# A hybrid scan kernel: the gate moved behind its slot's scan, the norm's variance a slot later, expert pairs packed one slot closer

## The chip, the cores and the metric

The kernel runs on one core of one Trainium2 chip, as one launch. The metric is the device time in microseconds, the median of several executions. The whole computation is in fp32.

## The reference, cut to what matters

The input is x of shape (2, 256, 64, 64): two batches, 256 channels, 4096 positions. Layer 0 adds to x a selective scan (Mamba) over the positions of the group-normed x. Layer 1 layer-norms the tokens, adds a forward and a backward Mamba with 512 inner channels each, and then adds a mixture of 8 experts: every expert is a three-layer MLP of 256 x 256 matrices with a batch norm and a ReLU behind the first two, and a softmax over the experts, computed from the mean of both batches, weighs them.

```python
# one Mamba, for inner channel d and state s
h = h * exp(dt[d] * A[d, s]) + dt[d] * x[d] * B[s]      # scan over positions
y[d] = sum_s h[d, s] * C[s] + x[d] * D[d]
out = (y * silu(z)) @ W_out
# experts
n = layernorm(t)                                        # over channels
t = t + sum_e w[f, e] * (relu(bn(relu(bn(n @ W1[e])) @ W2[e])) @ Wo[e])
```

## The kernel before, in words

Positions are cut into 8 chunks of T = 512. A job is one Mamba on one batch: layer 0 (256 inner channels, nj = 2 tiles of 128), the forward and the backward one of layer 1 (nj = 4). The six jobs follow one another, batch 0 first; 48 steps (a job and a chunk) in all. The backward job walks the chunks from 7 to 0.

The scan is done in quads. A quad g covers one tile of 128 channels and 4 of the 16 states, laid out as 128 partitions times 4 groups of 512 positions. There are 640 quads; 8 quads (n = 0 to 7, two channel tiles of 4 quads) make a group. Every quad has two halves h, and each half is one **slot**: 1280 slots in all, 16 to a step of layer 0 and 32 to a step of layer 1. In a quad POOL multiplies dt x by B (`emit_b`, L654, into a buffer bq, of which there are six); ACT computes the decay da into PSUM (L664, a slot ahead, two buffers); DVE runs the recurrence over half a quad (`emit_scan`, L690); the product with C is made by DVE (`emit_times_c`, L699) or, for the quads n = 0, 2, 5 and in every second group half of n = 4, by POOL (L714 copies the carried state, L715 multiplies); PE then sums the states into y (`emit_sum`, L723), which frees bq. y has a single PSUM buffer: it is opened by a matmul with the skip weights D (`emit_skip`, L730) and closed by the gate on DVE (`emit_gate`, L742), which writes y silu(z) into sz. `SUMS` gives the slots (n, h) in which the quads of a group are summed; -1 is the last quad of the group before.

The order on every engine is the order in which the main loop issues, slot by slot. In each slot it issues, in this order: DMAs on SP, (before the change) the gate, the skip, prepared matmuls ("pe"), the sums, expert matmuls ("pe2"), the carries and the next decay on ACT, prepared ACT work, the scan, prepared DVE work ("dve"), the C product, and POOL's work. Work around the scan is put into slots by hand: `SLOTS` says how many slots ahead of a step its input projection, convolution, x projection, softplus (dt) and z are made. `norm` and `features` spread a layer norm over slots: mean on PE, centre on DVE, squares on ACT, variance on PE (L804 in `features`), a root on ACT (L179, L180), a product on DVE (L809), a store on SP. `features` does this for the experts' norm, one chunk at a time, behind each step of a backward job, and notes in `ready` from which slot the chunk's experts may run.

An expert **pair** here is one expert on one chunk of one batch. `experts` plans as many pairs as fit into the scan stage: it walks the slots, counts the matmuls that PE and the activations that ACT have in each (`sl.count`, `sums_in`, `PE_ROOM`, `ACT_ROOM`), and places each layer's two output halves (L912 matmul, L921 or L923 eviction) where there is room. `follows` gives the earliest slot: a layer's next pair may start some slots behind the last use of the layer's weights, whose tile ew has one buffer. The load of the next weights (L932) is put on SP three slots behind that last use. Results go to DRAM as u (L942).

Behind the scan stage comes the tail. Pairs that were not done early run there on PE, chunk after chunk (L1201 for the first two layers, L1220 for the third, summed over experts in PSUM), each weighed on DVE (L1212) before its third layer. For each chunk there is side work, spread over the pairs of the chunk ahead of it: load n (L1086), add both batches (L1108), logits on PE (L1115), the softmax, the broadcast of the weights wb (L1146), the bias (L1163, L1164, L1166), and for each early pair a load of u (L1170), a product with its weight (L1171) and an addition to x (L1172) on DVE; the finished chunk is stored (L1175). The side work of the first chunk starts at its third pair.

Of the kernel before, what the change touches and what calls it, by code (L numbers as in the profile page):

```python
# [49 lines left out]
KC = C // P  # L50
# [11 lines left out]

POOL_HALF = (4, 0)

SUMS = {(0, 0): (-1,), (2, 0): (0, 1), (4, 0): (2, 3), (5, 1): (4,), (7, 0): (5, 6)}
POOL_AT = {0: "b3", 1: "c0 b4", 2: "b5", 3: "c2 b6", 4: "b7", 5: "h4 b8", 6: "c5 b9", 7: "b10"}
HUGE = 1e37

# [63 lines left out]
def hybrid_kernel(ctx: ExitStack, tc: tile.TileContext, a: dict, out: bass.AP):  # L132
    nc = tc.nc
# [11 lines left out]
    one_col, eps3, eps5, eps10, huge = (columns[:, k : k + 1] for k in range(5))  # L145
# [22 lines left out]
    nf_dram = [drp.tile([P, NCH, KC, T], F32, name=f"nf_dram{b}") for b in range(NB)]  # L168
# [9 lines left out]
    def rsqrt(dst, src, eps, scale=1.0):  # L178
        nc.scalar.activation(dst, src, AF.Ln, bias=eps, scale=scale)  # L179
        nc.scalar.activation(dst, dst, AF.Exp, scale=-0.5)  # L180
# [5 lines left out]
    with ExitStack() as st:  # L186
# [30 lines left out]
        sl = Slots()  # L217
# [467 lines left out]
        def emit_scan(g, h):  # L685
            i, j, sg = at(g)
            job, c = steps[i]
            d = da[g, h].rearrange("p q t -> p (q t)")
            b = bq[g][:, 2 * h : 2 * h + 2, :].rearrange("p q t -> p (q t)")
            nc.vector.tensor_tensor_scan(  # L690
                b if on_pool(g, h) else d, d, b,
                job.h[:, j, sg, 2 * h : 2 * h + 1] if c else 0.0, ALU.mult, ALU.add,
            )
# [46 lines left out]
        def emit_gate(i, j):  # L740
            sz = cks[i]["sz", j]
            nc.vector.scalar_tensor_tensor(sz, y.pop((i, j)), 0.5, sz, ALU.mult, ALU.mult)  # L742
# [38 lines left out]
        def features(b, c, v, s0):  # L781

            featured.add((b, c))

            def mean():
                v["ps"] = psp.tile([P, T], F32, tag="ps", name=f"fmean_{b}{c}")
                for k in range(KC):
                    nc.tensor.matmul(
                        v["ps"], mean_w, v["x"][:, k, :], start=(k == 0), stop=(k == KC - 1)
                    )  # L790

            def centre():
                v["cen"] = wk.tile([P, KC, T], F32, tag="cen", name=f"fcen_{b}{c}")
                nc.vector.tensor_tensor(v["cen"], v["x"], over_channels(v["ps"]), ALU.subtract)

            def square():
                for k in range(KC):
                    v["sq", k] = wk.tile([P, T], F32, tag="th", name=f"fsq_{b}{c}{k}", bufs=3)
                    nc.scalar.activation(v["sq", k], v["cen"][:, k, :], AF.Square)

            def variance():
                v["var"] = psp.tile([P, T], F32, tag="ps", name=f"fvar_{b}{c}")
                for k in range(KC):
                    nc.tensor.matmul(  # L804
                        v["var"], mean_w, v["sq", k], start=(k == 0), stop=(k == KC - 1)
                    )

            def divide():
                nc.vector.tensor_tensor(v["cen"], v["cen"], over_channels(v["var"]), ALU.mult)  # L809

            for d, queue, fn in (
                (0, "pe", mean), (1, "dve", centre), (2, "act", square), (3, "pe", variance),
                (4, "act", lambda: rsqrt(v["var"], v["var"], eps5)), (5, "dve", divide),
                (6, "sp", lambda: nc.sync.dma_start(nf_dram[b][:, c, :, :], v["cen"])),
            ):
                sl.put(s0 + d, queue, fn)
            sl.count(s0, 2, 0, (1,))
            sl.count(s0 + 1, 0, 2)
            sl.count(s0 + 3, 2, 2, (2,))
            ready.append((s0 + 8, b, c))  # L820

        def scales():

# [23 lines left out]
        def experts():  # L847

            last = 2 * nq - 6
            banks = sorted(sl.banks, key=lambda r: r[0])  # L850

            def fits(slot):

                at = sum(b[0] <= slot for b in banks)
                both = banks[:at] + [(slot, slot + 1, 0)] + banks[at:]
                return all(
                    both[k - 3][1] + both[k][2] <= both[k][0] for k in range(max(3, at - 2), min(len(both), at + 4))
                    if at in range(k - 3, k + 1)
                )

            def sums_in(slot):
                n, h = divmod(slot % 16, 2)
                return 1.25 * len(SUMS.get((n, h), ())) + (1 if (n, h) in ((1, 1), (5, 1)) else 0)

            todo = [(at, b, c, e) for at, b, c in sorted(ready) for e in range(E)]
            behind = act_behind = 0.0
            times = [[], [], []]

            def follows(l):

                k, m = divmod(len(times[l]), KC)
                if k == len(todo):
                    return None
                waits = [(l - 1, k * KC + 1, 2)] if l else []
                if m:
                    waits.append((l, k * KC, 0))
                elif k:

                    waits.append((l, k * KC - 1, 6 if l == 0 and todo[k][-1] == 0 else 5))
                    if l < 2:  # L880
                        waits.append((l + 1, k * KC - 1, 0))
                if any(n >= len(times[w]) for w, n, _ in waits):
                    return None
                return max([todo[k][0] + 3] + [times[w][n] + d for w, n, d in waits])

            for slot in range(last):
                behind = max(0.0, behind) + sl.products.get(slot, 0) + sums_in(slot) - PE_ROOM
                act_behind = max(0.0, act_behind) + sl.acts.get(slot + 1, 0) - ACT_ROOM
                for l in (2, 1, 1, 0, 0):
                    at = follows(l)  # L890
                    if at is None or slot < at:
                        continue
                    if behind + 2 > PE_BEHIND or act_behind + 1.3 > ACT_BEHIND or not fits(slot):
                        break
                    banks.insert(sum(b[0] <= slot for b in banks), (slot, slot + 1, 0))
                    times[l].append(slot)
                    behind += 2
                    act_behind += 1 if l == 2 else 1.3
            put = [
                (*item[1:], [times[l][k * KC + m] for l in range(3) for m in range(KC)])  # L900
                for k, item in enumerate(todo) if (k + 1) * KC <= len(times[2])
            ]
            emit_experts(put)
# [58 lines left out]
        ready = []  # L962
# [47 lines left out]
        done = []  # L1010
        for g in range(nq):
            i, jp, n = quads[g]
            for h in range(2):
                slot = 2 * g + h
                sl.run(slot, "sp")
                flush(slot)

                if (n, h) in ((1, 0), (5, 0)) and done:
                    emit_gate(*done.pop(0))

                if (n, h) in ((1, 1), (5, 1)):
                    emit_skip(i, 2 * jp + n // SG)
                sl.run(slot, "pe")
                for m in SUMS.get((n, h), ()):
                    if g - n + m >= 0:
                        emit_sum(g - n + m)
                sl.run(slot, "pe2")
                if (n, h) in ((0, 0), (4, 0)) and g:
                    done.append(at(g - 1)[:2])

                if slot:
                    emit_carry(*divmod(slot - 1, 2))
                emit_decay(*divmod(slot + 1, 2))
                if (n, h) in ((0, 0), (4, 0)):
                    emit_diagonal(i, 2 * jp + n // SG)
                sl.run(slot, "act")

                sl.run(slot, "dve0")
                emit_scan(g, h)
                sl.run(slot, "dve")  # L1040
                if not on_pool(g, h):
                    emit_times_c(g, h)

                if h == 0:
                    for what in POOL_AT.get(n, "").split():
                        m = g - n + int(what[1:])
                        if what[0] == "c":
                            emit_times_c_quad(m)
                        elif what[0] == "h":
                            if on_pool(m, 0):  # L1050
                                emit_times_c_quad(m, SG // 2)
                        else:
                            want_b(m)
                sl.run(slot, "pool")
            in_order()
# [335 lines left out]
```

## Time and profile before

| | |
|---|---|
| median of 3 runs | 5206.82 us (5206.63 to 5207.61) |
| the profiled execution | 5213.06 us |
| its span, first to last instruction | 5211.3 us |
| mean granted TensorE clock | 0.918 |
| busy: PE, DVE, ACT, POOL | 4298.0, 4584.8, 3681.8, 4410.2 us |
| scan stage | from about 44 us (first POOL product) to about 4542 us (last output projection) |
| tail | from 4545 us to the end |
| early pairs of 128 | 74 |

The durations in the profile are those of the profiled execution. Busy time is an average over stages with different limits, so a row of the windows view (one stretch of time, busy microseconds of PE, weight loads, DVE, ACT and POOL, then the clock, the DMA share and GB/s) is the view to start from. A number in square brackets in the timeline is the time for which the engine had been idle just before the instruction, and what ended that.

### The profile page before, as it was taken

The page shows a single profiled execution, that of the slowest core. Times are in us where ns is not written, and L with a number is a line of the kernel's source. Part 1 is how long each engine was busy: PE and PEld are TensorE (multiplying, and loading weights), DVE is VectorE, ACT ScalarE, POOL GpSimd, SP SyncE. Part 2 cuts the span into 40 slices and gives each one's busy share as a digit, 9 for nine tenths or more (in the row PEclk, how much of TensorE's full clock was granted, in tenths as well). Part 3 has the DMA queues.
Part 4 walks back from the last instruction along what each step waited for, and adds up shares of the span by engine and source line. Part 5 has one row for each costly group of instructions (what it writes and reads, how often), then busy time and mean ns, then how long its engine had stood idle before and what let it go on. Part 6 is the DMA issues. An engine that isn't in the chain of part 4 may idle for free. (4 is left out here: it accounts for less than half of the span.)

```text
span 5211.3 us, 47295 instructions
## 1 busy us (share of the span) xinstructions
PE 4298.0 (82%) x14920; PEld 1488.2 (29%) x14920; DVE 4584.8 (88%) x3083; ACT 3681.8 (71%) x7462; POOL 4410.2 (85%) x1438
## 2 busy tenths in 40 slices
PE   5777666766668888888888888888999989689999
PEld 1222212222222333332222332322333333234444
DVE  6998999999999999998989999999999999746333
ACT  5777777777767888887887888788788888522332
POOL 5998999999999999998989999999999999611010
PEclk8778888888889999999999999999999999899999
DMA  4444433344434554555555544445544455354322
GB/s 175 146 165 164 162 134 126 130 156 148 140 135 159 187 186 166 181 174 185 197 177 182 178 169 169 164 159 194 184 171 163 163 184 178 115 194 154 111 103 77
DMA packets 314731, 834.47 MB, mean 160 GB/s; under 512 B 35240, under 2 KB 102064, under 8 KB 272496
## 3 DMA queue, kind: packets, MB, share of 16 engines
q1 hardware_dynamic: 310768, 806.15, 44.5%
q0 software_dynamic: 3712, 25.30, 1.2%
q8 instruction: 118, 1.93, 0.1%
q14 instruction: 133, 1.09, 0.1%
HBM read 647.18 MB, written 184.16 MB: 160 GB/s over the span
## 5 line engine op out<-in xcount | busy, mean ns | idle before, releaser
L654 POOL TENSOR_TENSOR bq<-rxdt,bc 128x2048 f32<-128x2048 f32 x640 | 2892.9, 4542 | 34.8 <-issue 17.4
L664 ACT ACTIVATE da<-rdt,w_a 128x512 f32<-128x512 f32 x2560 | 1756.8, 686 | 113.6 <-DVE bq L690 67.8
L690 DVE TENSOR_TENSOR_SCAN da<-da,h_state,bq 128x1024 f32<-128x1024 f32 x664 | 1559.5, 2349 | 38.7 <-ACT da L664 27.3
L715 POOL TENSOR_TENSOR bq<-bq,bc 128x2048 f32<-128x2048 f32 (+1 forms) x280 | 1179.6, 4213 | 22.5
L723 PE MATMUL y<-bq,stack 128*32 128x512 f32 x5120 | 779.4, 687 | 362.1 <-POOL bq L715 337.2
L690 DVE TENSOR_TENSOR_SCAN bq<-da,h_state,bq 128x1024 f32<-128x1024 f32 x456 | 1052.3, 2337 | 27.9 <-ACT da L664 27.8
L699 DVE TENSOR_TENSOR bq<-da,bc 128x1024 f32<-128x1024 f32 x760 | 928.2, 1221 | 18.7
L912 PE MATMUL e<-eh,ew 128*128 128x512 f32 x1184 | 582.4, 621 | 60.5 <-DVE sp L513 20.5
L709 ACT COPY h_state<-da 128x2 f32<-128x2 f32 x759 | 119.3, 157 | 687.5 <-DVE bq L699 685.4
L675 ACT ACTIVATE bq<-h_state,bq,a 128x1 f32<-128x1 f32 x1120 | 429.9, 384 | 0.5
L723 PEld LDWEIGHTS y<-bq,stack 128*32 128x32 f32 x5120 | 144.9, 118 | 935.1 <-POOL bq L715 458.6
L1205 ACT ACTIVATE h<-hp,of,sc 128x512 f32<-128x512 f32 x216 | 167.7, 777 | 345.0 <-PE hp L1201 328.5
L414 PE MATMUL xs<-nx,w_in 128*128 128x512 f32 x640 | 320.1, 630 | 36.8 <-DVE xc L466 20.7
L414 PE MATMUL z<-nx,w_in 128*128 128x512 f32 x640 | 326.2, 638 | 23.7 <-DVE sp L513 16.9
L912 PEld LDWEIGHTS e<-eh,ew 128*128 128x128 f32 x1184 | 212.4, 193 | 422.3 <-issue 194.5
L912 PE MATMUL e<-en,ew 128*128 128x512 f32 x592 | 290.5, 622 | 47.3 <-DVE fcen L809 21.5
L452 PE MATMUL conv<-xs,w_conv 64*64 64x512 f32 x2560 | 320.5, 608 | 4.6 <-DVE sp L513 3.7
L761 PE MATMUL o<-sz,w_out 128*128 128x512 f32 x640 | 306.7, 620 | 0.0
L923 ACT ACTIVATE eh<-e,of,sc 128x512 f32<-128x512 f32 x296 | 223.7, 769 | 37.9 <-PE e L912 36.7
L517 POOL TENSOR_TENSOR xdt<-sp,xc 128x512 f32<-128x512 f32 x160 | 203.4, 1275 | 53.3 <-DVE sp L513 53.3
L501 PE MATMUL dt<-dbc,w_dt 64*128 64x512 f32 x320 | 197.2, 701 | 44.5 <-ACT dbc L488 27.7
L730 PE MATMUL y<-xc,w_d 128*128 128x512 f32 x320 | 181.0, 649 | 60.8 <-DVE sz L742 51.3
(138 smaller groups left out, 5043.0 us busy)
## 6 DMA issues: line engine op xcount, KB each, us to landing
rxdt<-xdtd SPq DMA_DIRECT2D x160, 1024.0 KB, 6.4
rdt<-dtd SPq DMA_DIRECT2D x160, 1024.0 KB, 6.3
bc<-bcd SPq DMA_DIRECT2D x384, 256.0 KB, 3.2
dtd<-sp SPq DMA_DIRECT2D x160, 256.0 KB, 3.5
xdtd<-xdt SPq DMA_DIRECT2D x160, 256.0 KB, 3.4
ew<-in_W SPq DMA_DIRECT2D x148, 256.0 KB, 4.8
u<-eu SPq DMA_DIRECT2D x74, 512.0 KB, 3.5
u<-u SPq DMA_DIRECT2D x74, 512.0 KB, 4.0
```

The source lines that it names most:

```text
L414: nc.tensor.matmul(ps, job.w["in", half][:, k, j * P : (j + 1) * P], rhs, start=(k == 0), stop=(k == KC - 1),)
L452: nc.tensor.matmul(v[r][64 * col : 64 * col + 64, :], job.w["conv"][rows, 2 * jp + j, k, :], ck["xs", jp][rows, j, k : k + T] if k < 4 els ...
L654: nc.gpsimd.tensor_tensor(bq[g], ck["rxdt", j], over_groups(ck["bc", 0, sg]), ALU.mult)
L664: nc.scalar.activation(da[g, h][:, k, :], cks[i]["rdt", j][:, q, :], AF.Exp, scale=steps[i][0].w["a"][:, j, q * SG + sg : q * SG + sg + 1],)
L675: nc.scalar.activation(bq[g][:, q, 0:1], job.h[:, j, sg, q : q + 1], AF.Identity, scale=cks[i]["a0", j][:, h, sg : sg + 1], bias=bq[g][:, ...
L690: nc.vector.tensor_tensor_scan(b if on_pool(g, h) else d, d, b, job.h[:, j, sg, 2 * h : 2 * h + 1] if c else 0.0, ALU.mult, ALU.add,)
L699: nc.vector.tensor_tensor(bq[g][:, two, :], d, cks[i]["bc", 1, sg].rearrange("p (o t) -> p o t", o=1).to_broadcast([P, 2, T]), ALU.mult,)
L715: nc.gpsimd.tensor_tensor(b, b, cks[i]["bc", 1, sg].rearrange("p (o t) -> p o t", o=1).to_broadcast([P, groups, T]), ALU.mult,)
L723: nc.tensor.matmul(y[i, j][q * CG : (q + 1) * CG, :], stack, bq[g][:, q, :], start=False, stop=(sg == SG - 1),)
L761: nc.tensor.matmul(v[m], job.w["out"][:, j, m * P : (m + 1) * P], ck["sz", j], start=False, stop=(j == job.nj - 1),)
L912: nc.tensor.matmul(ps, ew[l][:, k, m * P : (m + 1) * P], key[x][:, k, :], start=(k == 0), stop=(k == KC - 1),)
L923: nc.scalar.activation(key[dst][:, m, :], key["ps", l, m], AF.Relu, bias=of[:, l, e, m : m + 1], scale=sc[:, l, e, m : m + 1],)
```

## The change

Four edits, all of them in the order of work:

1. `emit_gate` is issued behind `emit_scan` of its slot, not at the slot's start. The skip, which opens y again, goes from slots (1, 1) and (5, 1) to (2, 0) and (6, 0), and the sum of quad 4 goes with it; `sums_in` follows.
2. In `features` the variance stands two slots behind the squares instead of one. Root, product, store and the slot from which the chunk is ready move by one.
3. In `follows` a layer's next pair may start four slots behind the last use of its weights, not five (six stays where a new chunk begins).
4. What the planner makes of it: 77 pairs are done early instead of 74. Three more pairs of chunk 6 of batch 1 (experts 2, 3 and 4) leave the tail, so that chunk has 3 pairs left there instead of 6, and 13 additions of early results instead of 10.

```diff
-SUMS = {(0, 0): (-1,), (2, 0): (0, 1), (4, 0): (2, 3), (5, 1): (4,), (7, 0): (5, 6)}
+SUMS = {(0, 0): (-1,), (2, 0): (0, 1), (4, 0): (2, 3), (6, 0): (4,), (7, 0): (5, 6)}
...
-                (0, "pe", mean), (1, "dve", centre), (2, "act", square), (3, "pe", variance),
-                (4, "act", lambda: rsqrt(v["var"], v["var"], eps5)), (5, "dve", divide),
-                (6, "sp", lambda: nc.sync.dma_start(nf_dram[b][:, c, :, :], v["cen"])),
+                (0, "pe", mean), (1, "dve", centre), (2, "act", square), (4, "pe", variance),
+                (5, "act", lambda: rsqrt(v["var"], v["var"], eps5)), (6, "dve", divide),
+                (7, "sp", lambda: nc.sync.dma_start(nf_dram[b][:, c, :, :], v["cen"])),
...
-            sl.count(s0 + 3, 2, 2, (2,))
-            ready.append((s0 + 8, b, c))
+            sl.count(s0 + 4, 2, 2, (2,))
+            ready.append((s0 + 9, b, c))
...
-                return 1.25 * len(SUMS.get((n, h), ())) + (1 if (n, h) in ((1, 1), (5, 1)) else 0)
+                return 1.25 * len(SUMS.get((n, h), ())) + (1 if (n, h) in ((2, 0), (6, 0)) else 0)
...
-                    waits.append((l, k * KC - 1, 6 if l == 0 and todo[k][-1] == 0 else 5))
+                    waits.append((l, k * KC - 1, 6 if l == 0 and todo[k][-1] == 0 else 4))
...
-                if (n, h) in ((1, 0), (5, 0)) and done:
-                    emit_gate(*done.pop(0))
-
-                if (n, h) in ((1, 1), (5, 1)):
+                if (n, h) in ((2, 0), (6, 0)):
                     emit_skip(i, 2 * jp + n // SG)
...
                 emit_scan(g, h)
+
+                if (n, h) in ((1, 0), (5, 0)) and done:
+                    emit_gate(*done.pop(0))
                 sl.run(slot, "dve")
```

## The prediction, made before the changed kernel ran

> **What bounds the kernel now.** I read the windows view first, cut by stage: the rows give length, then busy time of PE, weight loads, DVE, ACT and POOL.
>
> ```profile
> 40.00:560.00 520.00, 367.17 (x1302) 107.66 (x1302) 459.85 (x301) 376.49 (x768) 471.84 (x152) 0.80 0.48 166
> 560.00:1650.00 1090.00, 755.19 (x2893) 232.39 (x2895) 1067.34 (x700) 787.82 (x1652) 1084.25 (x345) 0.85 0.40 143
> 2230.00:2740.00 510.00, 444.89 (x1582) 147.58 (x1580) 456.95 (x295) 415.95 (x835) 456.95 (x145) 0.96 0.54 185
> 3700.00:4480.00 780.00, 703.79 (x2518) 245.20 (x2510) 759.66 (x488) 628.01 (x1298) 769.11 (x244) 0.96 0.50 173
> 4660.00:4760.00 100.00, 91.14 (x218) 38.95 (x217) 73.18 (x62) 26.62 (x36) 15.54 (x11) 0.98 0.51 176
> ```
>
> There are three regimes. In the layer-1 scans (second and fourth row) POOL is busy 99% and DVE 97 to 98%: POOL's multiplications set the pace, one step of 32 slots every 109.5 us, and a stall of PE or ACT costs nothing. In the two layer-0 scans (40:560, 2230:2740) POOL is at 90% and DVE at 88 to 90%: neither is full, so somebody waits on the path. After about 4545 PE works through the remaining expert pairs. Next, who waits in the first layer-0 scan (engine, line, releaser, us in total, times, longest), and below it the whole run:
>
> ```profile
> POOL h_state L714 <- DVE bq L690: 15.8, 11, 2.0
> DVE sz L742 <- PE y L723: 16.5, 7, 4.7
> ...
> DVE sz L742 <- PE y L723: 45.4, 37, 4.7
> PEld fvar L804 <- ACT fsq L799: 77.6, 30, 5.1
> PE fvar L804 <- ACT fsq L799: 57.8, 16, 4.3
> ```
>
> The gate (L742) holds DVE's queue until PE has summed y; the scan behind it is late, and POOL's product, which reads that scan, waits too. The timeline shows it:
>
> ```profile
> 218.25 0.69 DVE L742 SCALAR_TENSOR_TENSOR sz<-y,sz 128x512 f32<-128x512 f32 x1 [2.73 <-PE y L723]
> 218.86 4.58 DVE L690 TENSOR_TENSOR_SCAN bq<-da,h_state,bq 128x1024 f32<-128x1024 f32 x2
> 223.51 0.19 POOL L714 COPY h_state<-bq 128x4 f32<-128x4 f32 x1 [1.48 <-DVE bq L690]
> ```
>
> The reader should see that this pair is the only place where a wait that the change touches reaches the engine that sets the pace.
>
> The tail is read from its timeline:
>
> ```profile
> 4627.95 2.33 POOL L1108 TENSOR_TENSOR nm<-n,n 128x1024 f32<-128x1024 f32 x1 [12.24 <-DMA n<-nf_dram]
> 4662.14 3.36 DVE L1172 TENSOR_TENSOR x<-x,u 128x1024 f32<-128x1024 f32 x1 [8.01 <-POOL x L1166]
> 4677.93 1.23 DVE L1171 TENSOR_TENSOR u<-u,wb 128x1024 f32<-128x1024 f32 x1 [5.37 <-DMA u<-u]
> 4691.19 5.40 PE L1220 MATMUL y<-h,Wo 128*128 128x512 f32 x8 [3.64 <-DVE h L1212]
> ```
>
> Between 4590 and 4710 DVE, adding the early pairs' results (L1171 and L1172, 1.22 + 1.23 us a pair), holds PE, not the other way round.
>
> **What the Trainium skill says.** "PSUM — Partial Sum Buffer", Engine vs sequencer instructions: the queues of ScalarE, VectorE and GpSimd are strict FIFO. The trace agrees: the scan behind the gate at 218.25 starts only after it. "SBUF — State Buffer", Who interferes with whom: a DVE instruction with two SBUF inputs contends with a GpSimd one that reads SBUF. It agrees in the tail (the L1172 add takes 3.36 beside POOL, 1.23 alone); in the scan stage DVE reads one operand from PSUM, and POOL's product keeps 4.54. "DMA: Bandwidth & Descriptors", Issuing engines are not separate DMA queues: all issuers share the 16 DMA engines; that matters for the tail below. "Perfetto Trace Analysis", Optimization Strategy: the most contended engine may differ by regime; the windows say so here.
>
> **The change part by part.**
> *Gate behind its slot's scan.* No instruction is added. DVE runs scan, gate instead of gate, scan, so y gets one scan (2.35 us) more; a stall s becomes s - 2.35 or nothing. The stalls of the first layer-0 scan in the timeline are 4.73, 2.56, 2.73, 1.37, 2.13, 2.67 and 0.34: 16.5 in all, 3.3 left, 13.2 saved. In the second they are 1.00, 1.17, 4.03, 2.60 and 0.34: 9.1, 1.9 left, 7.2 saved. The other 25 (20 us) lie where POOL is full, or at the end: the last gate (2.05) is issued outside the loop and stays. POOL waits on DVE for 15.8 us in the first scan and 28.4 in the second, so there is room for the gain to arrive; ACT, the next in line (10.9 us of DVE's waits for da in the first), takes some. I count 11 and 5 (0 to 13.2, 0 to 7.2), and 1 for the rest (0 to 4). Behind the moved gate stand the slot's C product (1.22) and the next scan: they come 0.68 later than the scan, no later than before.
> *Skip (L730) one slot on, sum of quad 4 with the skip.* The skip must follow the gate, which is later by a scan; a slot is about 3.46 us, so PE's wait there (51 + 25 us for L742) does not grow. In layer 0 the sum now stands behind the convolution (40 matmuls, 4.5 us): its bq buffer comes free some 8 us later. POOL takes that buffer after a C product and a B product of another quad, 9 us; so nothing, at worst 1 us on each of 16 steps if PE is late. I take 0.5 in all.
> *Variance two slots behind its squares.* PE waited for the squares 77.6 us as the loader, of which 57.8 are matmul idle (the same stretches, not a sum). In layer-1 scans POOL covers that: 0 us, except at the very end, where the norm's last DVE step waited 1.62 on it; I count 1. The square's buffers (tag th) are held a slot longer: ACT's softplus waited 14.4 us in 9 for them and may wait as much again, covered by ACT's own waiting for DVE (685 us at L709); 0, at worst 5. The store and the read of that norm move one slot on SP; its first reader is a pair that the planner places after it.
> *Next pair four slots on instead of five: 77 pairs early, not 74.* Into the scan stage go 3 x 24 traced matmuls (0.43 us apart, 31 us of PE), 3 x 6 evictions on ACT (four of 0.77, two of 0.57: 12.7 us) and 12 DMAs on SP. PE has 76 us idle in 3700:4480, 25 of them the very wait for the squares that goes (in 3800:4400); ACT has 152. Cover: POOL. The weights' tile has one buffer: its load is issued three slots behind the last use, lands in 4.6 us (median), and the next use came two slots after the issue, now one. By the two plans 23 of 228 loads are that tight; each may hold PE 1 to 3 us, some 45 us of PE, and whatever SP queues behind the load waits for PE as it does now (231 us at L932). Hidden in layer 1; in layer 0 a handful count: 1.5 (0 to 8).
> *In the tail* three pairs go: 4.29 + 2.84 + 3.43 = 10.6 us each in the chain, 31.7 in all. I count none of it. Chunk 6 keeps 3 pairs, and all its side work (13 adds, not 10, and the routing of chunks 7 and 5) is now issued in one piece between its third pair and chunk 5. Routing of chunk 5 hangs on its n, which POOL sums at 4627.95 after the same DMAs as before; so PE can't begin chunk 5 before about 4636 (it began at 4646.4): 10 us instead of 31.7. Then DVE: three adds more (7.3) and a weighing fewer before chunk 5's first add, which until now waited 8.0 for POOL. 7.3 - 1.1 - 8.0 = -1.8, but x of chunk 5 is loaded behind the additional u and four weight loads, and the broadcast wb now meets the u loads on the shared DMA engines: +1 to +5. Net +1 (-2 to +6). From the weighing ahead of 4691.19 on, order and work are as before.
>
> Sum: -11 - 5 - 1 + 0.5 - 1 + 1.5 + 1 = **-15.0**. Against the profiled execution (span 5211.3, 5213.06 with what lies around it) 5198.1; the median shown is 6.2 below that, so **5192**, 0.29% under 5206.82.
>
> **Rivals.**
> *Tail counted in full.* If PE set the tail, 31.7 would come on top: 5160. PE is busy 91 of 100 us in 4660:4760, which speaks for it; the 3.64 ahead of 4691.19 and the missing pairs to fill 4604 to 4636 speak against. Half of it gives 5176.
> *No gain.* ACT takes the gate's place in layer 0 (it already ends 13.8 us of DVE's waits in the first): -0 to -8, 5199 to 5207. The 2.35 us of freed DVE time usually end in POOL's waits for DVE, which speaks against.
> *Slower.* PE falls behind in the last layer-1 scan: it is 90% busy there, gets 21 us more and most of the tight reloads. It decides once PE's 76 idle us are used up, so that y comes later than the gate's extra 2.35 us; then each of 16 steps loses about 1.5 us: +24, with 9 of the layer-0 gain left, is 5222. The load there, 21 us and a third of the 45, stays under half of the 76, so I give it little.
>
> **How the numbers follow.** Main case 0.62 (5184 to 5200, likeliest 5192); tail at least half 0.12; no gain 0.14; slower 0.12. The range 5174 to 5210 takes in the half tail and the no-gain case. A measurement of this kernel tells about 0.2% (10.4 us) from no change: the main case is faster by more in four fifths (0.50), with the tail 0.62, and a part of the middle 0.02: faster 0.64, same 0.25, slower 0.11.
>
> **What would show it.** L742's wait in 40:560 falls from 16.5 to about 3, in 2230:2740 from 9 to 2, POOL's wait at L714 falls with it, and the scan stage ends some 16 us earlier. The waits at L804 nearly vanish without a gain in layer 1: the step stays at 109.5 us. The time from the last scan to the end stays within a few us of now, with PE idle between 4604 and 4636 and again ahead of chunk 5's second y. It is wrong if the tail shortens by 20 us or more, if the layer-1 step changes, or if L912 waits for its weights by tens of us while POOL waits with it.

## The result, and the profile after

The changed kernel takes **5185.24 us** (median of 5 runs, 5181.76 to 5189.58) against 5206.82. The ratio is 0.9955, 95% interval 0.9943 to 0.9967, so it is 0.45% faster. The profiled execution took 5185.24 us, its span 5183.5. The forecast of 5192 (5174 to 5210) holds it. In good part that is luck: the gain of gate and variance and the cost of the packing were both put far too low, and the two errors, of opposite sign, met in the sum. The experiments separate them.

The windows view of the changed kernel, in the columns of before (length, busy time of PE, weight loads, DVE, ACT and POOL, clock, DMA share, GB/s):

```profile
40.00:560.00 520.00, 368.28 (x1338) 117.20 (x1337) 470.94 (x309) 382.27 (x783) 482.19 (x154) 0.82 0.49 167
2230.00:2740.00 510.00, 441.99 (x1582) 148.11 (x1582) 469.17 (x306) 428.87 (x857) 473.79 (x154) 0.96 0.56 191
3700.00:4480.00 780.00, 699.14 (x2496) 244.53 (x2497) 752.72 (x482) 625.42 (x1301) 763.30 (x242) 0.96 0.51 172
```

POOL is busier in both layer-0 scans (482.19 instead of 471.84 us, 473.79 instead of 456.95), which is where most of the time came from. In the last layer-1 scan it is *less* busy than before (763.30 of 780, was 769.11), which the main case of the prediction did not allow for. The granted clock there is 0.96 as before, so it is not the clock. The waits in the first layer-0 scan (waiting engine and line, releaser, us in total, times, longest):

```profile
POOL h_state L714 <- DVE bq L690: 9.7, 6, 2.1
...
DVE sz L742 <- PE y L723: 3.0, 3, 2.5
```

The gate's wait fell from 16.5 to 3.0, as worked out. POOL's wait for the scan fell by less, from 15.8 to 9.7. Of the gate's fall only what reaches POOL can be time of the kernel, as POOL sets the pace: these 6.1 us, and 10.3 if all that POOL stood idle in the stretch is counted (its busy time rose by that much). The same pair of instructions as before, in the timeline:

```profile
215.33 0.69 DVE L742 SCALAR_TENSOR_TENSOR sz<-y,sz 128x512 f32<-128x512 f32 x1
...
219.37 0.19 POOL L714 COPY h_state<-bq 128x4 f32<-128x4 f32 x1
```

The 2.73 us ahead of the gate and the 1.48 ahead of POOL's copy are gone. One wait of the whole run:

```profile
PE fvar L804 <- DVE sp L513: 55.8, 11, 5.3
```

PE's wait at the variance (L804) did not vanish. It waited 57.8 us for ACT's squares before; it now waits 55.8 us for DVE's L513.

To see where along the program time is won or lost I list the start of every 16th or so gate (L742; there are 160, the last one right behind the loop) minus the start of the same gate in the profile of before, and the time from the last gate to the end. Gates 1 to 16 are those of the first layer-0 scan, 81 to 96 those of the second, 97 to 128 those of batch 1's forward job and 129 to 160 those of its backward job, the last scan.

| kernel | gate 16 | 76 | 96 | 112 | 128 | 144 | 160 | last gate to end, us |
|---|---|---|---|---|---|---|---|---|
| before | 0 | 0 | 0 | 0 | 0 | 0 | 0 | 679.7 |
| changed | -8.6 | -13.3 | -28.7 | -31.1 | -28.6 | -24.4 | -24.3 | 676.2 |
| gate only | -11.7 | -13.7 | -25.0 | -27.2 | -25.7 | -28.6 | -29.3 | 677.9 |
| variance only | -4.6 | -3.8 | -12.6 | -13.0 | -10.0 | -12.0 | -15.7 | 682.7 |
| packing only | -3.7 | 0.0 | -0.2 | +2.5 | +5.0 | +4.2 | +4.1 | 678.1 |
| gate and variance | -9.8 | -12.8 | -26.8 | -30.4 | -30.4 | -33.0 | -37.3 | 674.0 |

The rows below the second are those of the first four experiments. The profiled execution of before was a long one (6.2 us above its median), and "variance only" and "packing only" have its program up to gate 16: some 4 us of every row there are run to run. Ten kernels of this document have the moved gate and the same program up to gate 16; there they lie on average 10.0 us ahead of before (8.5 to 11.7), the three without it 2.8 (0 to 4.6), so the move is worth about 7 us in the first scan. Later columns are best read against each other, and to some 3 us only. The changed kernel wins 15.4 us between gates 76 and 96 (a later kernel, which differs from it in the tail alone, wins 11.9) and then gives 4.3 back between 128 and 160, the last scan, where gate and variance without the packing win 6.9 more.

The tail is 3.5 us shorter, for three pairs fewer. Its timeline:

```profile
4577.35 3.58 PE L1115 MATMUL lt<-wr,nm 128*128 128x8 f32 x16 [8.67 <-POOL nm L1108]
...
4600.14 2.33 POOL L1108 TENSOR_TENSOR nm<-n,n 128x1024 f32<-128x1024 f32 x1 [11.85 <-DMA n<-nf_dram]
...
4602.53 3.58 PE L1115 MATMUL lt<-wr,nm 128*128 128x8 f32 x16 [18.85 <-POOL nm L1108]
...
4608.66 5.71 PE L1201 MATMUL hp<-n,W 128*128 128x512 f32 x8
...
4666.37 5.94 PE L1220 MATMUL y<-h,Wo 128*128 128x512 f32 x8 [7.05 <-DVE h L1212]
```

PE stands 8.67 and 18.85 us for the sum of both batches' n, begins chunk 5 at 4608.66, and then waits for DVE's weighing (4.35 us at 4646.77, 7.05 at 4666.37), which stands behind the additions.

### The profile page after: what moved, and what is told of

Read it like the earlier page. It is cut to its first block, busy times and chain, and to the rows that moved or that the text cites. A ratio compares the mean times of both kernels' runs of the same rounds, so it can differ in the third digit from the quotient of the medians.

```text
span 5183.5 us, 47326 instructions
## 1 busy us (share of the span) xinstructions
PE 4289.2 (83%) x14920; PEld 1486.0 (29%) x14920; DVE 4580.7 (88%) x3086; ACT 3678.8 (71%) x7468; POOL 4409.0 (85%) x1438
## 4 chain that ended last, share of the span: by engine, by line
DVE 20%; PE 15%; ACT 9%; issue 4%; POOL 4%; DMA 2%; SPq 0%; DVEq 0%; POOLq 0%; ACTq 0%
DVE da L690 10%; PE hp L1201 6%; DVE bq L699 5%; ACT da L664 4%; PE y L1220 3%; DVE bq L690 2%; POOL bq L654 2%; PE e L912 2%; PE conv L452 1%; POOL bq L715 1%; ACT bq L675 1%; PE y L723 1%; ACT eh L923 1%; DVE xc L466 1%; DMA u<-u 1%
## 5 line engine op out<-in xcount | busy, mean ns | idle before, releaser
L690 DVE TENSOR_TENSOR_SCAN bq<-da,h_state,bq 128x1024 f32<-128x1024 f32 x456 | 1059.3, 2338 | 28.5 <-ACT da L664 28.4
L723 PE MATMUL y<-bq,stack 128*32 128x512 f32 x5120 | 761.1, 688 | 329.3 <-POOL bq L715 304.6
L912 PE MATMUL e<-eh,ew 128*128 128x512 f32 x1232 | 604.1, 621 | 69.2 <-DVE sp L513 13.5
L414 PE MATMUL z<-nx,w_in 128*128 128x512 f32 x640 | 322.9, 637 | 19.3 <-DVE sp L513 11.9
L730 PE MATMUL y<-xc,w_d 128*128 128x512 f32 x320 | 194.8, 694 | 54.2 <-DVE sz L742 53.9
L690 DVE TENSOR_TENSOR_SCAN da<-da,bq 128x1024 f32<-128x1024 f32 x96 | 219.5, 2286 | 6.3 <-ACT da L664 3.6
```

The lines of the kernel that those rows point to most:

```text
L414: nc.tensor.matmul(ps, job.w["in", half][:, k, j * P : (j + 1) * P], rhs, start=(k == 0), stop=(k == KC - 1),)
L690: nc.vector.tensor_tensor_scan(b if on_pool(g, h) else d, d, b, job.h[:, j, sg, 2 * h : 2 * h + 1] if c else 0.0, ALU.mult, ALU.add,)
L723: nc.tensor.matmul(y[i, j][q * CG : (q + 1) * CG, :], stack, bq[g][:, q, :], start=False, stop=(sg == SG - 1),)
L912: nc.tensor.matmul(ps, ew[l][:, k, m * P : (m + 1) * P], key[x][:, k, :], start=(k == 0), stop=(k == KC - 1),)
```

## The experiments

Theory after the result: gate and variance gain in the layer-0 scans, the packing loses in the last layer-1 scan because of its evictions (the activations by which ACT takes the experts' results out of PSUM), and the tail is held by its side work. Rivals: the tight reload of weights (the load lands only just before its use), the mere amount of expert work, or PE's pairs in the tail. Ratios are to runs of the kernel before on the same chip; "gain" is what the ratio lacks to 1, times 5206.8.

**Each part alone, and two together.** The first takes edit 1 of the change, the second edit 2, the third edit 3 with the number of pairs fixed, the fourth edits 1 and 2.

```diff
 # third kernel
-                    waits.append((l, k * KC - 1, 6 if l == 0 and todo[k][-1] == 0 else 5))
+                    waits.append((l, k * KC - 1, 6 if l == 0 and todo[k][-1] == 0 else 4))
...
-            ]
+            ][:77]
```

> Only the gate, the skip and the sum of quad 4 are moved; 74 pairs as before. Theory (the gate's stall in the layer-0 scans pays): nearly the whole gain is here. The first layer-0 scan gets about 11 us shorter, the second at least 7, the layer-1 scans and the tail stay within 3 us: 5185 to 5190. Rival (the variance's wait or the packing pays in the second layer-0 scan, where the changed kernel gained 13 us): the first layer-0 scan gains 11, the second under 4: 5193 to 5197.

Measured: 5182.77 us, ratio 0.9948 (0.9931 to 0.9964), a gain of 27 us (19 to 36), more than expected. The layer-1 scans do not stay within 3 us: between gates 16 and 76, and 96 and the last, it wins 6.3.

> Only the variance of the experts' norm is two slots behind its squares; 74 pairs. Theory: PE's wait at L804 goes, POOL covers it, so 5203 to 5208; at most 2 us come from the end of the scan stage. Rival (the wait at L804 is what held PE, ACT and then the gate at the start of the second layer-0 scan): 4 to 9 us less, 5198 to 5203, all of it between 2240 and 2740 us.

Measured: 5200.3 us, ratio 0.9983 (0.9976 to 0.9990), a gain of 9 us (5 to 12). The rival of the expectation holds.

> Only the packing, four slots instead of five, cut off at 77 pairs. Theory: three pairs leave the tail, and the tail gets only 2 to 5 us shorter, because n of the next chunk and the additions on DVE hold it; in the scan stage they cost 0 to 8 us: 5202 to 5212. Rival (a pair moved is worth its 10.6 us on PE): 5175 to 5185.

Measured: 5214.67 us, ratio 1.0012 (1.0005 to 1.0018): a loss of 6 us (3 to 9), outside the 5202 to 5212 expected. None of it comes from the last scan (between gates 128 and 160 it wins 0.9): it loses 3.7 between gates 16 and 76 and 5.2 between 96 and 128. Its plan puts the pairs into other slots than that of the changed kernel.

> Gate and variance, five slots as before: the planner makes 73 pairs. Theory: like the changed kernel without its packing; the layer-0 gains are kept, the about 6 us that the changed kernel loses in the last layer-1 scans do not appear, and the tail with a pair more is 0 to 3 us longer than before: 5180 to 5187. Rival (the loss in the last layer-1 scans comes from the later variance holding the squares' buffers): that loss of about 6 us stays, 5187 to 5193.

Measured: 5169.42 us, ratio 0.9923 (0.9908 to 0.9938), a gain of 40 us, far more than expected. The loss in the last scan does not appear, though the variance is moved here too, so the squares' buffers are not its cause. The packing therefore costs the full change about 16 us (5185.24 - 5169.42), more than it costs alone; 11.2 of them lie between gates 128 and 160.

What the variance moves is two places. The first: the norm of batch 0's last chunk falls into the first slots of batch 1's layer-0 scan, where POOL isn't full. The timeline of the kernel before there:

```profile
2392.40 1.28 ACT L179 ACT_TABLE_LOAD   x1
2393.70 0.66 ACT L179 ACTIVATE fvar<-fvar,columns 128x512 f32<-128x512 f32 x1
...
2394.38 1.28 ACT L180 ACT_TABLE_LOAD   x1
...
2396.16 0.59 ACT L776 COPY xr<-o 128x512 f32<-128x512 f32 x1
...
2396.81 1.19 PE L759 MATMUL o<-xr,ident 128*128 128x512 f32 x2 [3.62 <-ACT xr L776]
...
2402.45 4.54 POOL L654 TENSOR_TENSOR bq<-rxdt,bc 128x2048 f32<-128x2048 f32 x1 [6.15 <-PE y L723]
...
2403.27 0.69 DVE L742 SCALAR_TENSOR_TENSOR sz<-y,sz 128x512 f32<-128x512 f32 x1 [4.03 <-PE y L723]
```

ACT makes the norm's root with two table loads; xr stands behind it in ACT's queue; PE waits 3.62 us for xr, and the sums behind it in PE's queue come late, so that POOL waits 6.15 for a buffer and the gate 4.03 for y. With the variance alone moved, the timeline has:

```profile
2391.65 4.54 POOL L654 TENSOR_TENSOR bq<-rxdt,bc 128x2048 f32<-128x2048 f32 x1 [0.41 <-PE y L723]
...
2392.46 0.69 DVE L742 SCALAR_TENSOR_TENSOR sz<-y,sz 128x512 f32<-128x512 f32 x1 [1.63 <-PE y L723]
```

POOL's wait fell by 5.7 us. The table agrees: variance only wins 8.8 us between gates 76 and 96. The second place is the last norm of all, at the end of the loop, which the prediction named. POOL's last wait for a scan, in the kernel before:

```profile
4515.53 0.19 POOL L714 COPY h_state<-bq 128x4 f32<-128x4 f32 x1 [3.83 <-DVE bq L690]
```

and with the variance alone moved:

```profile
4499.86 0.19 POOL L714 COPY h_state<-bq 128x4 f32<-128x4 f32 x1 [1.45 <-DVE bq L690]
```

The last eight gates take 2.5 us less with the variance alone moved, 0.2 less with the gate alone. In this kernel a tail 3 us longer takes that back.

**The last three pairs back in the tail.** The changed kernel, with

```diff
                 if (k + 1) * KC <= len(times[2])
-            ]
+            ][:74]
```

> The changed kernel with its early pairs cut at 74, so that the last three go back to the tail; the four-slot rule stays for the other 74. If the pairs hardly matter to the tail (theory, from the gate-and-variance kernel with 73 pairs, whose tail was 674.0 us against 676.2 with 77), the time stays within 4 us of the changed kernel's 5185, and the stretch from the last gate in the loop to the end within 3 us of 676. If each pair costs its 10.6 us of the chain there (rival), it is 31 us slower, about 5216. If the three pairs that were put last are what holds up the last layer-1 scan, its last gate comes some 7 us earlier and the time falls to about 5178.

Measured: 5182.14 us, ratio 0.9947 (0.9930 to 0.9963), last gate to end 679.7 us. The pairs are worth 3.5 us of tail, not 31.7. Taking them out of the scan stage gave 4.4 us at its end (last gate at 4502.89 instead of 4507.27). The changed kernel has there:

```profile
4477.27 3.75 PE L912 MATMUL e<-eh,ew 128*128 128x512 f32 x4 [6.99 <-DMA ew<-in_Wo]
...
4491.20 0.19 POOL L714 COPY h_state<-bq 128x4 f32<-128x4 f32 x1 [4.30 <-DVE bq L690]
```

PE stands 6.99 us for weights of the last pair; the variance is behind it in PE's queue, root and product come late, and POOL waits 4.30 us for the scan behind them, 1.10 in the cut. By these two traces a reload does cost at this one place, about 3 us; it was not tried apart from its pair. Up to gate 154 the cut lay within 2.2 us of the changed kernel, so the rest of the loss in the last layer-1 scan is not these pairs'.

**Evictions or reloads.** In both kernels below the planner leaves a slot after placing one half of a layer there, so that ACT never has two expert evictions in one slot. The first keeps the four slots, the second has five and so no tight reload.

```diff
                     act_behind += 1 if l == 2 else 1.3
+                    break
```

> The changed kernel with the four-slot rule kept, but the planner places at most one half of a layer in a slot, so that no slot has two or three expert evictions on ACT (68 have two and 2 have three in the changed kernel). It gets 69 pairs early, with 22 of their weights reloaded in the tight four slots (23 in the changed kernel). Read by the last gate in the loop, which lay at 4507 in the changed kernel and at 4494 with the five-slot rule. Theory (two evictions in a row on ACT make a decay late): the last gate comes at 4494 or earlier. Rival (the tight reload holds PE): it stays at 4505 to 4509. The tail has eight pairs more; up to the first four they were free, four more may cost 15 to 42 us, so the whole is expected at 5185 to 5215 whatever the verdict on the scan.

Measured: last gate at 4494.94; 5230.34 us, ratio 1.0044 (1.0029 to 1.0059).

> Gate and variance as changed, five slots between pairs, and at most one half of a layer in a slot: 66 pairs early, no tight reload and no two evictions in a slot. With the kernel before it this makes a square: evictions together or not, reload tight or not. Theory (evictions): the last gate lies with that of the one-eviction kernel with four slots, within 4 us, and before that of the gate-and-variance kernel (4494). Rival (reload): it lies with the gate-and-variance kernel, 10 us or more before the one-eviction kernel with four slots. The tail has 11 pairs more than the changed kernel's: 30 to 75 us longer, the whole 5195 to 5245.

Measured: last gate at 4491.34; 5232.96 us, ratio 1.0048 (1.0033 to 1.0063).

The scan is decided: with 22 tight reloads and no two evictions together the last gate (4494.94) lies where it lies without tight reloads (4494.33 for gate and variance, 4491.34 here). The reload is out as the cause of what every step loses. The tails are a miss on the upper side: 734.1 us for 69 pairs early, where I had expected 15 to 42 us on 676.2. With 69 pairs chunk 6 keeps all eight of its pairs, and PE is nearly full there; the window of the one-eviction kernel:

```profile
4600.00:4700.00 100.00, 96.32 (x230) 41.24 (x228) 40.18 (x37) 28.42 (x38) 10.07 (x7) 0.98 0.33 120
```

PE has 96.32 us busy of 100 in place of 81.57 in the changed kernel. The eight pairs cost about 58 us of tail (734.1 instead of 676.2), but the three more of the second kernel only another 5.7: what a pair costs there depends on what PE waits for beside it. These two kernels also have 8 and 11 pairs fewer in the scan, so the amount of work was still a rival.

**Evictions or amount of work.** As the first of them, but only from slot 1024 on, which is the last layer-1 scan:

```diff
                     act_behind += 1 if l == 2 else 1.3
+                    if slot >= 1024:
+                        break
```

> The changed kernel with the four-slot rule, at most one half of a layer in a slot from slot 1024 on (the last layer-1 scan), and free before. It has 74 pairs early and 21 tight reloads, so it stands against the cut at 74 with the same number of pairs and, but for two, of tight reloads; what differs is that one slot of the last scan has two evictions on ACT instead of 17. Theory (two evictions ahead of a decay): up to the gate at about 3630 it runs with the changed kernel, and from there to the last gate it loses nothing: last gate at 4493 to 4497, DVE's wait for da at L690 under 6 us in that scan, the whole 5171 to 5177. Rival (the amount of expert work, or the tight reload): last gate at 4502 to 4507 as in the cut at 74, the whole 5180 to 5186.

Measured: 5174.81 us, ratio 0.9933 (0.9918 to 0.9948); last gate at 4495.06, 7.8 us before that of the cut at 74 with the same number of pairs. At gate 128 it was 1.7 us ahead, so 6.1 come from the last scan. The waits of POOL and DVE from 3630 to 4400, in the cut at 74:

```profile
POOL h_state L714 <- DVE bq L690: 12.1, 10, 1.5
...
DVE bq L690 <- ACT da L664: 11.0, 7, 2.1
...
DVE da L690 <- ACT da L664: 6.5, 9, 1.8
```

and with the evictions spread:

```profile
DVE bq L690 <- ACT da L664: 8.5, 5, 2.6
...
POOL h_state L714 <- DVE bq L690: 4.7, 5, 1.5
...
DVE da L690 <- ACT da L664: 1.4, 2, 1.2
```

POOL's wait falls by 7.4 us, about those 6.1. The expectation named 6 us for DVE's first wait; it is 8.5, but three quarters of the second wait went too (17.5 to 9.9 together). Sorted by what ACT did since the decay before, 9.2 of the 17.5 us stand behind two or more expert evictions and 8.3 behind one or none; with the evictions spread it is 0 and 9.9. So the number of pairs is out: the part behind evictions that stand together went, and the rest stayed. How it looks, in the timeline of the changed kernel:

```profile
3968.93 1.41 ACT L664 ACTIVATE da<-rdt,w_a 128x512 f32<-128x512 f32 x2
3970.27 0.58 ACT L436 COPY xs<-xs 128x512 f32<-128x512 f32 x1
...
3970.98 0.58 ACT L921 COPY eu<-e 128x512 f32<-128x512 f32 x1
3971.46 0.78 ACT L923 ACTIVATE eh<-e,of,sc 128x512 f32<-128x512 f32 x1
...
3974.37 1.42 ACT L664 ACTIVATE da<-rdt,w_a 128x512 f32<-128x512 f32 x2 [1.79 <-DVE bq L690]
...
3975.82 2.35 DVE L690 TENSOR_TENSOR_SCAN bq<-da,h_state,bq 128x1024 f32<-128x1024 f32 x1 [1.48 <-ACT da L664]
```

Between two decays stand an input projection's eviction and two of the experts'. The next decay then starts only once DVE's running scan is done, and the next scan is 1.48 us late. The same stall stands at 3865.03, 4195.75 and 4306.34. But it doesn't need two expert evictions. With the evictions spread three scans from 3740 on are as late behind that of an input projection and one of an expert, among them:

```profile
4077.64 2.35 DVE L690 TENSOR_TENSOR_SCAN bq<-da,h_state,bq 128x1024 f32<-128x1024 f32 x1 [1.49 <-ACT da L664]
```

ACT had then been idle for 1.81 us until DVE's running scan was done. And two expert evictions without an input projection's cost the gate-and-variance kernel only 0.32 us at a time (4187.80 in its trace). So it also counts in which slots the evictions stand; the spread kernel has them in other slots as well as apart, and the two were not tried one by one. Why that decay waits for the scan as well, and not only for ACT, was not tried on its own.

**The order of the tail's side work.** In the first tail chunk the routing (n, sum, logits, weights) of both next chunks, 7 and 5, goes ahead of the additions:

```diff
-            for j in whole[at : at + 1] + after:
-                ahead += routes(j)
+            soon = [routes(j) for j in whole[at : at + 1] + after]
+            for part in (slice(0, 1), slice(1, 2), slice(2, 4), slice(4, 5)):
+                for r in soon:
+                    ahead += r[part]
```

> The changed kernel with the side work of its first tail chunk in another order: the routing of both following chunks (7 and 5) is issued ahead of the additions of early results. It tests what holds the tail after three of its pairs went. Theory (PE stands 8.67 and 18.85 us for POOL's sum of both batches, because the second chunk's n is loaded and summed behind the first chunk's additions): the two waits fall to under 10 us together and the time falls 8 to 15 us, to 5170 to 5177. Rival (DVE's additions set the start of the tail whatever PE has): PE waits for the weighed h on DVE instead, and the time stays within 3 us of 5185.

Measured: 5172.3 us, ratio 0.9933 (0.9918 to 0.9948), and 664.0 us from last gate to end. PE in the tail:

```profile
4584.11 3.58 PE L1115 MATMUL lt<-wr,nm 128*128 128x8 f32 x16 [3.35 <-POOL nm L1108]
...
4619.98 5.39 PE L1220 MATMUL y<-h,Wo 128*128 128x512 f32 x8 [5.83 <-DVE h L1212]
...
4653.37 5.76 PE L1220 MATMUL y<-h,Wo 128*128 128x512 f32 x8 [8.71 <-DVE h L1212]
```

The 18.85 us became 3.35, and 12.2 us of the tail went with it. The other wait is 8.67 as before, so the two sum to 12.0, not under 10. Part of the saving became longer waits for DVE's weighing (5.83 and 8.71, from 4.35 and 7.05).

**The best versions.** The spread evictions with this order, and gate and variance with it. ("The kernel before" in the first text is the one with the spread evictions.)

> The kernel before with the routing of both next chunks ahead of the additions in the tail. If the two gains lie in different stages, they add: the changed kernel's tail fell by 12.2 us with that order at 3 pairs in the first tail chunk. With 6 pairs there PE has more to do meanwhile, so I expect 3 to 10 us from it: 5163 to 5172. If PE's own work sets this tail with 6 pairs, nothing is gained: 5171 to 5177.

Measured: **5162.79 us**, ratio 0.9910 (0.9895 to 0.9925); last gate to end 665.4 instead of 679.7. With 12 us this is more than the 3 to 10 expected.

> The gate-and-variance kernel (five slots, 73 pairs) with the same order in the tail. Its tail was 674.0 us, with PE waiting little before 4651 and then 3.3 and 2.2 us for the weighed h: 3 to 8 us are expected, so 5160 to 5167; nothing (5169) if DVE's additions set it whatever comes first.

Measured: 5165.91 us, ratio 0.9919 (0.9902 to 0.9935); last gate to end 672.3. Its interval overlaps that of gate and variance alone, and the tail fell by only 1.7: in this kernel, with seven pairs in the first tail chunk, the order hardly matters. The first of the two is the fastest kernel run, faster than the changed kernel (its interval lies below 0.9943).

## Why the prediction was right, and where it was not

| step | predicted, us | measured, us |
|---|---|---|
| gate and skip, first layer-0 scan | -11 | about -7 (mean of ten traces less mean of three) |
| gate, second layer-0 scan | -5 | -11.3 (gates 76 to 96) |
| gate, elsewhere, with skip and sum | -0.5 | -6.3 (gates 16 to 76, and 96 to the last) |
| variance | -1 | -9 (-5 to -12) |
| packing in the scan | +1.5 (0 to 8) | +6 alone with the tail, about +16 on the rest |
| tail | +1 (-2 to +6) | -3.5 (within the packing's) |
| sum | -15.0 | -21.6 of the medians |

The measured column comes from several kernels and doesn't add up to its last row. Taken together, gate and variance were put at -17.5 and gave -40, packing and tail at +2.5 and cost 16.

**Mechanism of the gate: right; sizes wrong.** The gate's stall ended in POOL's wait for the scan. In the first scan the terms of L742 were counted too high: it fell by 13.5, but POOL's wait at L714 by 6.1. In the second the term was too low: POOL had 28.4 us of such waits there, and 20.5 with the gate alone, 7.9 less where 5 were counted; the rest of the 11.3 is about what two traces of one program differ by. And "the rest", 1, came to some 6: the layer-1 scans are not as closed as "POOL is busy 99%" says. In the last one POOL waited 6.7 us for the scan (3630 to 4400), and 4.1 with the gate alone moved.

**Variance: the step that failed is its cover.** "In layer-1 scans POOL covers that: 0 us" is true of those scans to within some 3 us (variance only loses 2.6 us between gates 96 and 128 and wins 3.2 between 128 and 152). But the norm of the last chunk of batch 0 runs in a layer-0 scan, where nothing covers it; the 4.03 us stall that I had put down to the gate was the end of that chain. The gate's pair is thus not "the only place" where a wait that the change touches reaches POOL. At the very end, for which 1 was counted, some 2.5 came. Gate and variance each remove most of that stall, so their gains in the second layer-0 scan (11.3 and 8.8) come to 14.0 together, not 20. On the whole the two together give no less than their sum (40 against 27 and 9), and that isn't explained here; with 73 pairs that kernel also has another plan.

**Packing: the step that failed is "Cover: POOL".** I added ACT's 12.7 us to 152 idle and PE's 31 to 76, and priced the reload. Sums of idle time say nothing of the order: evictions that stand together ahead of one decay make one scan late, with ACT 80% busy. The layer-1 step, which was to stay at 109.5 us, went to 110.3 in the last scan and to 108.8 without the packing (gates 128 to 152, six steps; before 109.5). The rival "slower" named the right place with the wrong engine: DVE never waits for y there (at L742, 3630 to 4500; 2.9 us before), so PE wasn't late with it, and a reload cost only at the very end, about 3 us. What in the order of the evictions makes the decay late stays open in part.

**Tail: right in its mechanism, outside its range.** None of the 31.7 us was to be counted, and 3.5 came, more than the -2 of the range. The start of chunk 5 was put at 4636, or 24.3 less by the earlier last gate, 4611.7; it was 4608.66. PE then waited for DVE's weighing as foreseen. The rival "tail in full" falls with the cut at 74; its half does too.

**Waits at L804: the reading failed.** They kept their size with another releaser (55.8 us, DVE's L513). L513 is the last reader of dt, and by the kernel's text dt and the variance take their PSUM tiles from the same buffers (tag ps), so it may be a buffer that PE waits for; that was not tried. In any case the gain of the variance does not come from these waits.

## What to carry to other kernels

Before a gain is put at nothing because an engine is full, look for the instances that run in another stage: one chunk's norm in another scan was worth more than all the others. For work that is moved beside a queue, count what stands together, slot by slot, ahead of the instruction that the pacing engine needs; idle time in sum does not show it. And what a shorter stage gives back is read from the pacing engine's wait (POOL at L714), not from the wait that the change removes.

## What was not expected of the hardware

Two table loads and two activations make ACT's queue unavailable for 3.85 us (2392.40 to 2396.25), and what stands behind that queue waits: PE stood 3.62 us for xr, and POOL 6.15 behind PE. The Trainium skill, "ScalarE: Activation LUTs", What ACT_TABLE_LOAD costs, gives about 1.28 us for the load and a drain of 1.38 beside it. The trace has the 1.28; the activation behind it starts 0.02 us later (2393.70), and 0.013 us in the median of the 115 loads of the trace of before, so the drain doesn't show there, and an estimate with the page's sum would be too high here.
